# A four-layer macaron network on one core: the third attention's products as single passes over parts, and the first batch's parts of two attentions sent in two steps

## The chip, the cores and the metric

The kernel runs on one core of one Trainium2 chip. The metric is the device time of one execution in microseconds (us). All four layers are one program, so the time is that of the whole network, and the edited stage is about a fifth of it.

## The reference

The state `x` has 4 x 512 x 128 values in f32. Each of four layers adds half a feed-forward block, an attention and the other half of a feed-forward block:

```python
x = x + 0.5 * L3_ffn(x)     # the pattern of every layer, here the last
x = x + L3_attn(x)
x = x + 0.5 * L3_ffn(x)
```

Layers 0 and 3 have mixtures of experts with a limited capacity, layers 1 and 2 other mixtures. The attentions of layers 0, 1 and 3 are softmax attentions with 16 heads of 8 values; layer 2 has a gated recurrence in that place. In the order of time, the attention of layer 0 is the first (its tiles end in `a0`), that of layer 1 the second (`a1`), that of layer 3 the third (`a3`). The edited one is the third:

```python
xn = (x - mu) / sqrt(var + eps) * gamma + beta
q, k, v = split(xn @ W_qkv.T + b_qkv)          # 16 heads of 8
scores = q @ k.T / sqrt(8)                      # 512 x 512 for each of 4 x 16 heads, no mask
out = x + (softmax(scores) @ v) @ W_out.T + b_out
```

The first attention has a causal mask and a bias that depends on the distance, the third has neither.

## The kernel before

**Stages.** The state stays on the core in four tiles `xs[b]` (one for each batch, 128 partitions x 4 tiles of tokens x 128). In the third layer, experts write their rows to a table in memory (`res_f`); `combine(b)` loads a batch's rows (`r_f`) and adds them to `xs[b]` (L548 group). `begin(b)` of the attention goes on from there: sums for the norm (`bn_stats`, `bn_aggr`), a power on POOL, the normed rows, four transposes on PE (called T in the prediction) into `nT`, then the products for q and k (`qk`), then those for v, which `values` copies from PSUM into `vpad`, a tile with the 8 values of each head and a column of ones that gives the sum of the softmax's denominators.

**Units.** `attention()` is one function for the first and the third. It runs 16 units (batch b, group g of four heads), one after the other. A head has a slot of 32 rows of the 128 (`SLOT`), and the four products of a unit's four heads run on four row groups of the PE array at once. `bank(...)` gives one of the eight PSUM banks (128 x 512 f32) in turn.

In the third attention a unit computes its scores twice. `largest` makes scores with queries on the partitions (`s_a`, L627) and DVE reduces each bank to the negated maximum of each row (`low<-s_a`, L726). `lowered` transposes these maxima on PE (`low_a`) and DVE adds them to q, giving `ql_a` (L735): q's slot then holds the query's 8 values, and in a row that k keeps at one, minus the maximum. `by_key` makes the scores again with keys on the partitions (`t_a<-ql_a,k_a`, L627), now with the maximum already taken off; ACT takes the exponential straight from the bank into `w_a` (L746), and `times_values` multiplies with `vpad` into `acc_a` (L842). `summed` copies the finished `acc_a` to `ou_a`, `normalized` transposes it (`ot_a`, L861) and divides, `gathered` and `ended` do the output projection (`proj_a`) of a batch and add it to `xs[b]` (`residual`).

**Order.** The order of PE, DVE, ACT and POOL inside `attention()` is written out by hand (`manual_schedule`). A unit is eight half-steps, each a round of two score products of a later unit and two products by key of the present one, taken alternately, with half of the value products behind it:

```python
together(step(largest, n + lead), step(by_key, n))
if of:
    times_values(*((0, NT - 2, 1) if of == (0, NT - 1) else (*of, 0)))
```

`lead = 2 * NT + 2` says that the scores are ten half-steps (one unit and two) ahead of the products by key. Around the rounds, `go_on()` and `begin_next(u)` advance a later batch's `begin(b)` and the routing of the next mixture (`lg`, `rank_f`) by one step at a time, so that these lie between the rounds. `start(u)` makes a unit's q and k, `fetch` (used by the first attention only) loads them. The first unit has an order of its own (`first_unit`), since nothing runs beside its first scores.

**q and k of a unit.** In the third attention `heads` makes q and k of a batch for all heads in an order in which each slot holds a head of each group; `unit_q` (ACT, L1024) and `project` (POOL, L1704) mask them to the unit's group with the constants `own` and `next_row`, and products are f32. In the first attention `split_heads` makes each of q and k as two parts, `hi` (rounded to the format FR, which PE reads in a single pass) and `lo` (the remainder). `to_units` writes the parts to memory as rows of 4 copies x 8 values for each head, in the orders

```python
halves = (0, 1, 0, 1), (0, 0, 1, 1)
```

for q and k, so that one product over a slot's 32 rows sums all four pairs of parts: eight DMAs for a batch (`qrows_a`, `krows_a`, L1091), and `unit_qk` fetches a unit's q and k (L1100). The first unit of the first attention takes another way (`first_qk`, straight from a product with repeated weights).

DMAs are issued on SP's queue unless another engine is named (`nc.scalar` is ACT's, `nc.gpsimd` POOL's).

## Time and profile before

| | us |
|---|---|
| three runs, median (lowest to highest) | 1475.67 (1471.78 to 1477.84) |
| the profiled execution's own time | 1481.44 |
| its span | 1479.7 |
| PE busy | 1231.3 (83%) |
| DVE busy | 889.6 (60%) |
| POOL busy | 693.9 (47%) |
| ACT busy | 680.3 (46%) |

The mean granted clock of PE is 0.907 of full speed. The stages of the profiled execution, read from tables of busy time by stretches (us):

| stretch | stage | PE busy | DVE | ACT | POOL | clock |
|---|---|---|---|---|---|---|
| 0 to 104 | first mixture | 78.5 | 37.8 | 35.9 | 55.8 | 0.98 |
| 104 to 121 | head of the first attention | 7.3 | 6.6 | 1.9 | 2.8 | 0.60 |
| 121 to 320 | its units | 180.5 | 154.1 | 156.6 | 160.5 | 0.97 |
| 970 to 1047 | mixture ahead of the third attention | 63.2 | 31.5 | 24.9 | 35.4 | 0.92 |
| 1047 to 1064 | head of the third attention | 7.3 | 4.5 | 4.3 | 7.4 | 0.50 |
| 1064 to 1357 | its units | 288.9 | 214.4 | 162.3 | 71.5 | 0.98 |
| 1357 to 1395 | its last projection and the next routing | 9.5 | 9.3 | 1.4 | 12.0 | 0.54 |
| 1395 to 1462 | last mixture | 62.9 | 29.4 | 25.4 | 29.9 | 0.95 |

How to read it: a row of a table of stretches gives the busy time of each engine with the number of instructions in brackets. A row of the timeline gives start, duration, engine, line of the kernel, operation, and output<-inputs, and in brackets how long the engine had waited and for whom. A group's row gives the total, the mean of one in ns, and the idle time ahead of it. Each engine runs its own instructions in the order written, and waits where an input is not there or an output's buffer is not free. L627 is the line of `product`, so products of scores and by key are told apart by their tiles.

### The profile page before, as it was taken

The page shows a single profiled execution, that of the slowest core. Times are in us where ns is not written, and L with a number is a line of the kernel's source. Part 1 is how long each engine was busy: PE and PEld are TensorE (multiplying, and loading weights), DVE is VectorE, ACT ScalarE, POOL GpSimd, SP SyncE. Part 2 cuts the span into 40 slices and gives each one's busy share as a digit, 9 for nine tenths or more (in the row PEclk, how much of TensorE's full clock was granted, in tenths as well). Part 3 has the DMA queues.
Part 4 walks back from the last instruction along what each step waited for, and adds up shares of the span by engine and source line. Part 5 has one row for each costly group of instructions (what it writes and reads, how often), then busy time and mean ns, then how long its engine had stood idle before and what let it go on. Part 6 is the DMA issues. An engine that isn't in the chain of part 4 may idle for free.

```text
span 1479.7 us, 27632 instructions
## 1 busy us (share of the span) xinstructions
PE 1231.3 (83%) x9882; PEld 770.7 (52%) x9882; DVE 889.6 (60%) x3109; ACT 680.3 (46%) x1434; POOL 693.9 (47%) x812
## 2 busy tenths in 40 slices
PE   5877999977979899989898688359599999997494
PEld 4554776765746566666564344237343434332273
DVE  5236888753356676776468867434488787771252
ACT  2334977852442477767521112123256655553041
POOL 5545878862524777777332113645421242213253
PEclk9997999996999999999999777579799999998597
DMA  8623333103433674420220810132100000000333
GB/s 260 193 58 107 123 105 108 38 18 104 123 81 103 177 254 137 140 84 17 58 58 1 301 44 12 34 103 73 39 16 8 9 15 2 15 1 16 79 85 109
DMA packets 109548, 122.40 MB, mean 83 GB/s; under 512 B 10038, under 2 KB 74788, under 8 KB 109412
## 3 DMA queue, kind: packets, MB, share of 16 engines
q1 hardware_dynamic: 97892, 103.22, 23.9%
q0 software_dynamic: 6656, 13.22, 2.7%
q10 hardware_dynamic: 4864, 4.20, 1.0%
q8 instruction: 79, 1.29, 0.3%
q14 instruction: 57, 0.47, 0.1%
HBM read 70.36 MB, written 50.24 MB: 82 GB/s over the span
## 4 chain that ended last, share of the span: by engine, by line
PE 62%; DVE 14%; POOL 8%; issue 7%; DMA 6%; ACT 3%; SPq 0%; POOLq 0%; ACTq 0%; DVEq 0%
PE s_a L627 11%; PE t_a L682 8%; PE h_f L496 5%; PE o_f L532 5%; PE acc_a L842 5%; PE acc_a L704 4%; DVE x L1588 3%; PE t_a L627 3%; PE gu_f L1356 2%; PE y_f L1557 2%; PE gu_f L1357 2%; POOL disp_f L422 2%; PE o_f L1391 2%; PE ot_a L861 2%; POOL res_f L518 2%
## 5 line engine op out<-in xcount | busy, mean ns | idle before, releaser
L669 POOL TENSOR_SCALAR sc_a<-sc_a,top_a 128x128 f32<-128x128 f32 (+3 forms) x256 | 275.9, 1092 | 74.9 <-DVE top_a L654 38.5
L627 PE MATMUL s_a<-k_a,q_a 32*128 32x512 f32 (+3 forms) x1280 | 239.6, 536 | 14.3 <-DVE top_a L658 6.6
L726 DVE TENSOR_REDUCE low<-s_a 128x1 f32<-128x512 f32 x256 | 163.1, 684 | 42.8 <-PE t_a L627 30.6
L746 ACT ACTIVATE w_a<-t_a 128x512 f32<-128x512 f32 x240 | 131.9, 596 | 108.8 <-PE t_a L627 72.2
L682 PE MATMUL t_a<-ident,sc_a 128*128 128x128 f32 x1280 | 170.8, 279 | 7.1 <-DVE top_a L658 6.5
L518 POOL DMA_INDIRECT res_f<-y_f,back_f x112 | 106.8, 953 | 135.5 <-ACT y_f L517 108.1
L682 PEld LDWEIGHTS t_a<-ident,sc_a 128*128 128x128 f32 x1280 | 142.4, 143 | 32.8 <-issue 12.0
L627 PE MATMUL t_a<-ql_a,k_a 32*128 32x512 f32 x480 | 159.0, 644 | 0.6 <-DVE low L726 0.4
L671 ACT ACTIVATE sc_a<-sc_a,top_a 128x128 f32<-128x128 f32 (+3 forms) x256 | 134.3, 577 | 17.8 <-DVE top_a L658 12.4
L627 PEld LDWEIGHTS s_a<-k_a,q_a 32*128 32x128 f32 x1280 | 84.9, 185 | 84.1 <-issue 45.8
L691 ACT ACTIVATE w_a<-t_a 128x256 f32<-128x256 f32 (+2 forms) x192 | 94.4, 527 | 60.8 <-PE t_a L682 60.1
L422 POOL DMA_INDIRECT disp_f<-n_f,to_f x96 | 95.1, 991 | 44.5 <-issue 32.4
L532 PE MATMUL o_f<-w_l,h_f 128*128 128x128 f32 (+1 forms) x896 | 110.2, 278 | 2.4 <-ACT h_f L500 2.3
L496 PE MATMUL h_f<-dT_f,w_l 128*128 128x320 f32 (+1 forms) x256 | 106.4, 554 | 2.8 <-ACT dT_f L474 2.8
L532 PEld LDWEIGHTS o_f<-w_l,h_f 128*128 128x128 f32 (+1 forms) x896 | 102.3, 184 | 11.4 <-ACT h_f L500 4.3
L704 PE MATMUL acc_a<-w_a,vpad 128*32 128x128 f32 x2560 | 97.5, 278 | 0.7 <-ACT w_a L691 0.6
L693 ACT COPY w_a<-t_a 128x256 f32<-128x256 f32 (+2 forms) x192 | 93.6, 528 | 5.8 <-PE t_a L682 5.8
L173 POOL TENSOR_SCALAR rs_f<-mv_f 128x4 f32<-128x4 f32 (+1 forms) x23 | 5.3, 232 | 184.5 <-DVE mv_f L170 184.3
L658 DVE CUSTOM_DVE_ANT_0 sc_a<-s_a,future 128x128 f32<-128x128 f32 (+3 forms) x128 | 62.3, 487 | 44.8 <-PE s_a L627 39.8
L517 ACT ACTIVATE y_f<-o_f,d_f 128x128 f32<-128x128 f32 (+1 forms) x112 | 39.0, 394 | 106.4 <-DVE o_f L512 99.6
L842 PE MATMUL acc_a<-w_a,vpad 128*32 128x256 f32 x1024 | 83.7, 398 | 2.3 <-ACT w_a L746 2.0
L1403 POOL TENSOR_TENSOR h_f<-h_f,cb_f 128x512 f32<-128x512 f32 x32 | 40.6, 1285 | 80.1 <-DVE h_f L1362 41.5
(366 smaller groups left out, 2210.1 us busy)
## 6 DMA issues: line engine op xcount, KB each, us to landing
fac_a<-fac_a_sb SPq DMA_DIRECT2D x36, 256.0 KB
disp_f<-zeros_f SPq DMA_DIRECT2D x4, 2080.0 KB
d_f<-disp_f SPq DMA_DIRECT2D x32, 260.0 KB
w_l<-in_L_ffn_w_dram SPq DMA_DIRECT2D x16, 512.0 KB
cb_f<-rows_f SPq DMA_DIRECT2D x16, 512.0 KB
q_a<-fac_a SPq DMA_DIRECT2D x32, 256.0 KB
k_a<-fac_a SPq DMA_DIRECT2D x32, 256.0 KB
r_f<-res_f SPq DMA_DIRECT2D x16, 256.0 KB
```

Source lines behind the costliest of these rows:

```text
L422: nc.gpsimd.indirect_dma_start(out=self.to[c][i0 + t][:, :], out_offset=bass.IndirectOffsetOnAxis(ap=to[:, c, t : t + 1], axis=0), in_=ns[ ...
L496: nc.tensor.matmul(ps[u][:, :cap], w1[:, e, (c + u) * P : (c + u + 1) * P], dT, start=True, stop=True)
L518: nc.gpsimd.indirect_dma_start(out=self.back[e * per + s][:, :], out_offset=bass.IndirectOffsetOnAxis(ap=back[:m, s : s + 1], axis=0), in_ ...
L532: nc.tensor.matmul(po[:m, s, :], h[:, c, s * P : s * P + m], w2[:, e, c, :], start=(c == 0), stop=(c == NC - 1),)
L627: nc.tensor.matmul(ps[:, n0:n1], q[r : r + SLOT, i * P : (i + 1) * P].bitcast(as_), k[r : r + SLOT, n0:n1].bitcast(as_), start=True, stop= ...
L669: nc.gpsimd.tensor_scalar(sc, sc, top, None, ALU.subtract)
L671: nc.scalar.activation(sc, sc, AF.Exp, bias=top, scale=-1.0)
L682: nc.tensor.transpose(ps[:, x * n + j * P : x * n + (j + 1) * P], st["sc", u, i, r0 + x][:, j * P : (j + 1) * P], ident,)
L704: nc.tensor.matmul(st["acc", u][r * SLOT : (r + 1) * SLOT, i * P : (i + 1) * P], vpads[b % 2][:, j, g * 4 + r, :], st["w", u, i, r][:, j * ...
L726: nc.vector.tensor_reduce(st["low", u][:, i, c : c + 1], ps, AX.X, ALU.max, negate=True)
L746: nc.scalar.activation(w, ps, AF.Exp)
L842: nc.tensor.matmul(acc[r * SLOT : (r + 1) * SLOT, n0:n1], vpads[b % 2][:, j, g * 4 + r, :], st["w", u, j, r, half] if ("w", u, j, r, half) ...
```

## The change

- **Units from the second on in parts.** The third attention uses the first's method: q and k of a batch come from the plain projection (`split_late`), as `x` (ACT), `hi` (ACT, for the first batch's q DVE) and `lo` (POOL, for the first batch's q DVE); `to_units` writes them to memory and `fetch` loads each unit's q and k, three units ahead. Score products and products by key are then single passes in FR. `unit_q`, the masked k, `heads`, `head_weights`, `own` and `next_row` go.
- **The largest in parts.** In a unit of parts q's slot is full, so minus the maximum can't be a row of it. `top_in_parts` splits the maxima into two FR parts in columns 0 and 1 of a slot of `low` (two small operations on DVE, one unit ahead); `lowered` copies the transposed tile into `less` on ACT in place of the addition on DVE; `by_key` adds to each bank a second product, of `twos` (ones in rows 0 and 1 of each slot) with `less`. `by_key_half`, used in the first unit only, stays as it was.
- **The first unit** stays f32, on q and k of its own (`first_plain`), whose weights are zero outside its rows, with a row of ones from the bias.
- **The order.** `lead` becomes `2 * NT + 4`; `first_unit` makes two more half-steps of scores and fetches unit 3; `top_in_parts(u + 1)` stands at the third step (j = 2) of unit u; `begin(b)` of the later batches gets two more yields.
- **Work that changes engine** in the third attention: the additions of `combine` (DVE to POOL for batches 1 to 3), the copies of v (DVE to ACT for batches 1 to 3; v's bias is now folded into the row `ob` by a product in the weights' preparation), the copy `oT` (to ACT).
- **Two steps.** For the first batch of the first and the third attention `to_units` writes group 1 first (eight DMAs of 64 KB, q's on SP's queue and k's on ACT's), then groups 2 and 3 (eight of 128 KB, on SP's); group 0 is not written. All other batches are written whole, as eight DMAs of 256 KB on SP's queue.

```diff
+        two = pool.tile([P, 2, P], FP, name="two", tag="two", bufs=1)
+        nc.gpsimd.memset(two[:, 0], 0.0)
+        for r in range(4):
+            nc.gpsimd.memset(two[r * SLOT : r * SLOT + 2, 0, :], 1.0)
+        nc.gpsimd.tensor_copy(two[:, 1].bitcast(FR), two[:, 0])
...
             for ps, r in out:
-                c = r * SLOT + (units[u][1] + 1) % NG * HD
-                nc.vector.tensor_reduce(st["low", u][:, i, c : c + 1], ps, AX.X, ALU.max, negate=True)
+                nc.vector.tensor_reduce(st["top", u][:, i, r : r + 1], ps, AX.X, ALU.max, negate=True)
+
+        def top_in_parts(u):
+            low = lows[u % len(lows)].rearrange("p t (r c) -> p t r c", c=SLOT)
+            hi, lo = (low[:, :, :, x] for x in range(2))
+            nc.vector.tensor_copy(hi.bitcast(FR), st["top", u])
+            nc.vector.tensor_tensor(lo, st["top", u], hi, ALU.subtract)
...
+            if in_parts(u):
+                st["less", u] = pool.tile([P, S], FP, name=f"less_{tag}{u}", tag="less", bufs=2)
+                nc.scalar.copy(st["less", u].bitcast(FR), ps)
+                return
...
-                yield lambda ps=ps, r=r: product(ps, k, st["ql", u], r * SLOT, j, 0, S)
+                yield lambda ps=ps, r=r: product(ps, k, q, r * SLOT, j, 0, S, as_, True)
                 out.append((ps, r))
+            for ps, r in out:
+                rows = slice(r * SLOT, (r + 1) * SLOT)
+                yield lambda ps=ps, rows=rows: nc.tensor.matmul(
+                    ps, twos[0][rows, :].bitcast(FR), st["less", u][rows, :].bitcast(FR), start=False, stop=True
+                )
...
-        lead = 2 * NT + 2
+        lead = 2 * NT + 4
...
+                        if j == 2 and nxt:
+                            top_in_parts(u + 1)
                         together(step(largest, n + lead), step(by_key, n))
...
+    def to_units(parts, tag, first=False):
+
+        out = [
+            dram.tile([NG, 4, 4, HD, S], FP, name=f"{name}rows_{tag}", tag=f"{name}rows_{tag}") for name in "qk"
+        ]
+        for g0, g1 in ((1, 2), (2, NG)) if first else ((0, NG),):
+            for (hi, lo), order, rows, queue in zip(parts, halves, out, (nc.sync, nc.scalar if g0 == 1 else nc.sync)):
+                for x in (0, 1):
+                    for c in (c for c in range(4) if order[c] == x):
+                        queue.dma_start(
+                            rows.rearrange("g h c d s -> c (g h) d s")[c, g0 * 4 : g1 * 4],
+                            (hi, lo)[x][g0 * SLOT : g1 * SLOT],
+                        )
...
-                qk[b] = to_units(split_heads(pool, nT, wT, bT, tag), tag, (nc.sync, nc.sync if b else nc.scalar))
+                qk[b] = to_units(split_heads(pool, nT, wT, bT, tag), tag, b == 0)
...
-                yield from summed(b)
+                yield from summed(b, nc.gpsimd if b else nc.vector)
...
-                    if t == 1:
+                    if t == 1 or b > 0 and t < NT - 1:
                         yield
...
-                qk[b] = heads(pool, nT, mixed, bT, tag)
+                if b == 0:
+                    whole_[:] = first_plain(pool, nT, first, tag)
+                rows[b] = to_units(split_late(pool, nT, wT, bT, tag, b == 0), tag, b == 0)
                 yield
-                values(b, nT, wvT, bv, tag)
+                values(b, nT, wvT, None, tag, b > 0)
```

The new function that makes the parts in the third attention (behind the products for q and k, `ps`):

```python
            nc.scalar.activation(x, ps[s], AF.Identity, bias=bT[:, s : s + 1])
            if first and s == 0:
                nc.vector.tensor_copy(hi.bitcast(FR), x)
            else:
                nc.scalar.copy(hi.bitcast(FR), x)
            (nc.vector if first and s == 0 else nc.gpsimd).tensor_tensor(lo, x, hi, ALU.subtract)
```

## The prediction

> **What bounds the kernel now.** I read the page first, then stretches of time, then single half-steps in order of time. The whole-span shares (PE 83%) are an average over stages, so I start from the stage that is edited: the third attention, from its first score product at 1063.7 us to its last value product at 1357 us. Busy us of each engine there (columns: start:end, length, PE, PEld, DVE, ACT, POOL, granted clock, DMA share, GB/s):

> ```profile
> 1270.00:1290.00 20.00, 19.79 (x157) 7.02 (x159) 13.42 (x23) 11.04 (x21) 10.19 (x11) 1.00 0.09 28
> 1290.00:1310.00 20.00, 20.00 (x183) 7.67 (x179) 15.58 (x29) 12.94 (x25) 0.00 (x0) 1.00 0.01 1
> 1310.00:1330.00 20.00, 20.00 (x171) 8.05 (x170) 15.47 (x39) 11.40 (x22) 3.84 (x10) 1.00 0.00 1
> 1345.00:1362.00 17.00, 12.83 (x72) 5.22 (x72) 1.79 (x5) 4.93 (x9) 2.40 (x3) 0.77 0.04 13
> ```

> PE is full at full clock, DVE stands at 13 to 16 of 20, ACT at 11 to 13. So PE's work sets the pace. The sixteen units (batch, group) end with a copy ou_a; those copies run from 1095.0 to 1357.0 us, so 15 units take 262.0 us, 17.5 us each. What a unit consists of, in the groups and then in one half-step (two score products and two products by key, on four row groups of the array at once):

> ```profile
> L726 DVE TENSOR_REDUCE low<-s_a 128x1 f32<-128x512 f32 x256 | 163.1, 684 | 42.8 <-PE t_a L627 30.6
> L746 ACT ACTIVATE w_a<-t_a 128x512 f32<-128x512 f32 x240 | 131.9, 596 | 108.8 <-PE t_a L627 72.2
> ```
> ```profile
> 1129.06 0.69 PE L627 MATMUL s_a<-k_a,q_a 32*128 32x512 f32 x1
> ...
> 1129.59 0.59 PE L627 MATMUL s_a<-k_a,q_a 32*128 32x512 f32 x1
> ...
> 1130.13 0.64 PE L842 MATMUL acc_a<-w_a,vpad 128*32 128x256 f32 x8
> 1130.22 1.29 DVE L726 TENSOR_REDUCE low<-s_a 128x1 f32<-128x512 f32 x2 [0.60 <-PE t_a L627]
> 1130.26 1.08 ACT L746 ACTIVATE w_a<-t_a 128x512 f32<-128x512 f32 x2 [0.80 <-PE t_a L627]
> ...
> 1130.70 0.69 PE L627 MATMUL s_a<-k_a,q_a 32*128 32x512 f32 x1
> ```

> Each f32 product is two instructions, 0.53 us apart, so a round of four products takes 1.07 us (1129.06 to 1130.13); the value products follow for 0.57 (to 1130.70). DVE and ACT wait for PE (0.60 and 0.80 in brackets). The first attention already runs its products in single passes, and shows what one costs:

> ```profile
> 211.27 0.45 PE L627 MATMUL s_a<-k_a,q_a 32*128 32x384 f32 x4
> 211.65 0.41 PE L379 MATMUL rank_f<-masks_f,not_before 128*128 128x32 f32 x2
> ...
> 215.22 0.51 PE L627 MATMUL s_a<-k_a,q_a 32*128 32x512 f32 x4
> 215.66 0.66 PE L682 MATMUL t_a<-ident,sc_a 128*128 128x128 f32 x4
> ```

> A round of four at 512 columns holds PE for 0.44 us (215.22 to 215.66), at 384 for 0.38. The slope, 0.055 per 128 columns, makes about 0.22 of pure streaming in 512.

> **The change part by part, stage sum first.** Per half-step PE loses 1.07 and gains 0.44 for the four products, plus the two new products of `twos` with `less` that add to the same banks. No row shows these. Below, they cost the stream alone, 0.22; above, a round of their own, 0.44. I take 0.31, since an f32 pair spends 0.53 on two double streams (0.44) and thus about 0.09 above its streaming. So 0.75 in place of 1.07.

> In the 262 us there are 118 half-steps with products by key (472 instructions t_a). Values take 120 x 0.57 = 68, the transposes ot_a and low_a 15 x 2 x 0.59 = 18, and PE's batch work (T, qk, v, proj, routing) and waits the remainder. Batch work by its rows: 5.8 qk, 3.5 v, 3.5 proj, 3.2 lg, with transposes and ranks about 22. That leaves 262 - 68 - 18 - 22 = 154 for products, or 1.30 a half-step: 1.07 and 0.23 of slips, of which the trace shows 0.25 in every other half-step (1127.17 to 1128.49 is 1.32, not 1.07). After: 118 x 0.75 = 89, so PE's floor is 89 + 68 + 18 + 22 = 197.

> DVE's floor: about 196 busy in these 262 us. Off go 14 additions ql_a (9.6), five batch sums of 0.84 moved to POOL (4.2), values and q of three batches (2.1 + 2.3), about 1.4 of copies; on come 14 splits of the largest, two small operations each, with 0.17 to 0.25 by the 0.16 to 0.26 us of DVE's other small rows: 5 to 7. About 183. ACT: 151 busy, minus 13 masked q (9.6), plus 14 copies `less` at 0.59 and for three batches some 2.8 each: 158. POOL loses 12 masked k (9.2) and gains about 12 additions at 1.27, and has room (0 to 10 of 20).

> PE and DVE now stand close, so waits between them count. Eight banks hold one sum and four products per half-step; in the built order the fourth product of every other half-step in the first half of a unit, and sometimes the third, waits for the reduce of the half-step before. A half-step starting at P has its first score in DVE's hands at P + 0.6, both reduced at P + 1.85 (two at 0.61 and a wake-up); a tight next round, due at P + 1.32, then finishes its products at about P + 1.85 + 0.55 rather than P + 2.07: about 0.35 late. With four tight ones per unit that is 1.4 a unit, 21 over 15: pace 197 + 21 = 218, or 14.5 a unit. Ends: 197 (no waits) and, all tight, two half-steps per 2.94 + 0.08, 8 x 1.51 + 1.2 + 1.5 = 14.8 plus DVE's 2.7 of other work not hidden, 17.5.

> **Queues and head of the third attention.** Batch 1 must be rearranged through DRAM before unit 4. In the built order only the v products and four half-steps, 1.0 + 4 x 1.45 = 6.8 us, stand on PE between its projection and its first use; unit 4 is started a half unit earlier than in the kernel before, which needed no DRAM trip here. In the first attention the same eight writes and the fetch run on SP so:

> ```profile
> 148.38 1.17 SPq L1091 DMA_DIRECT2D qrows_a<-qhi_a  x2
> ...
> 157.49 0.33 SPq L1100 DMA_DIRECT2D k_a<-krows_a  x1
> ```

> 9.1 us from first write to the fetch of k, about 2.5 more to land (writes to fetch in the same rows: 154.4 to 157.5 is 3.1), and 1.4 ahead for two ACT operations: 13.0. PE is blocked for 13.0 - 6.8 = 6 us, and everything queued behind it on PE (products by key, values) waits too; SP's next loads are for later units and don't matter. All later batches have one and a half units, 21 us, and are free. PE falls to a lower clock after such a gap: 130 to 160 us, behind the 6.44 below, has 0.85. I add 2. The head: four more projections of f32 ahead of the first scores, 1.9 us in the warm second set of the first attention (118.44 to 120.3), against 0.9 saved in v at the better clock: 1.4 in all. POOL's six small fills for `two` (0.2 each) follow its fills of low (974.81), after which POOL waits 13.87 us for the first expert anyway; without that wait, about 1 us. Total loss 9.4.

> **First attention, two steps.** PE waits here for unit 1:

> ```profile
> 134.35 0.48 PE L627 MATMUL s_a<-k_a,q_a 32*128 32x128 f32 x4 [6.44 <-DMA k_a<-krows_a]
> ```

> The wait for eight writes of 256 KB becomes one for eight of 64 KB, but eight more writes (128 KB) are issued on SP, 0.6 each, ahead of the fetch: it moves from 128.8 to about 127 at best 125. Gain 0 to 4.5, I take 2.5; next in line behind it is POOL, which is busy until 132.3.

> Sum: 262 - 218 = 44, minus 9.4, plus 2.5: 37 saved. The profiled execution took 1481.4 (span 1479.7 and 1.7 around), so 1444 by its clock; it lies 5.8 above the median of 1475.67, on which I forecast **1439**.

> [...] DVE's row above waits for PE, and in 1290 to 1310 it is 78% busy: it has a quarter to give. [...] And where PE waits, the clock counts: the row 1345 to 1362 has PE 75% busy at 0.77. [...]

> **Rivals.**
> (a) Emptying PSUM binds: all half-steps tight, part of DVE's other work unhidden, 16 us a unit. 262 - 240 = 22, minus 9.4, plus 2.5: 1461. For: DVE's floor of 183 is close to PE's 197, and waits in both directions. Against: the second half of each unit has banks to spare in the built order. Chance 0.2.
> (b) The products don't come in at one pass: the added pair costs a round of its own (0.44) and the old slips of 0.23 stay. 118 x (0.88 + 0.23) + 108 = 239: 1460. For: no row shows the pair; against: rounds of 0.44 in all ten units that I looked at. Chance 0.1.
> (c) Slower: PE's clock gives way in the stage. At clock c its floor is 197/c; with 9.4 lost and 2.5 won it passes 262 from c below 0.77. At 0.75 it is 263 plus waits of 10: 1475.7 + 273 - 262 + 6.9 = 1494. For: 75% busy goes with 0.77 above. Against: the first attention at 36.52 of 40 (200 to 240 us) keeps 1.00, and the after-stage should be 90% busy. Chance 0.1.
> (d) No waits at all: 197, so 1418. Chance 0.1.

> **Numbers.** The forecast has 0.5. About 0.5% (7.4 us) is what a measurement of this kernel can tell from no change. (a), (b) and (d) are faster by more than that, but for 0.08 that falls short through their upper ends (17.5 a unit): faster 0.82, same 0.08, slower 0.10. The range takes in (d) and the far side of (a): 1414 to 1468.

> **What would show it.** Right: ou_a copies about 14.5 us apart; reduce pairs of 1.29 back to back; `less` products adding about 0.3; PE blocked once for some 6 us by k_a<-krows_a of batch 1; the wait at 134.35 shorter by 2 or 3. Wrong: copies still 17 apart with PE waiting for DVE top_a (then a), full PE with longer rounds (b), or a clock under 0.9 in the stage (c).

## The result, and the profile after

The changed kernel takes 1465.27 us (median of 21 runs, 1446.72 to 1482.56) against 1475.67 (21 runs, 1468.56 to 1481.09): 10.4 us or 0.7% less by the medians, where 37 us (2.5%) were forecast. The ratio on record, 0.9885 (interval 0.9863 to 0.9906), leaves out eight of the changed kernel's 21 runs, those more than 1.5% above its fastest. The profiled execution took 1471.50 (span 1469.8), 9.9 less than that of before and 6.2 above the median.

The third attention's stretches after (columns as before; behind the engines stand granted clock, DMA share and GB/s); the last row is the stretch from the first copy ou_a to the last:

```profile
1120.00:1140.00 20.00, 13.35 (x106) 5.39 (x105) 10.01 (x18) 9.15 (x18) 7.42 (x6) 0.74 0.49 157
1140.00:1160.00 20.00, 20.00 (x142) 7.39 (x140) 12.61 (x26) 10.98 (x21) 0.00 (x0) 0.58 0.09 28
...
1280.00:1300.00 20.00, 20.00 (x205) 8.70 (x201) 17.67 (x34) 16.62 (x31) 0.83 (x1) 1.00 0.11 34
...
1320.00:1347.00 27.00, 26.96 (x151) 10.63 (x150) 2.85 (x15) 11.99 (x22) 8.20 (x10) 0.50 0.06 21
...
1103.06:1347.01 243.95, 232.54 (x1896) 100.83 (x1896) 169.36 (x407) 156.96 (x291) 72.82 (x106) 0.84 0.20 63
```

PE looks full in three of the first four rows, but the clock, 1.00 from 1074 to 1350 us in the profile before, stands at 0.58 and 0.50 in two of them. The copies ou_a run from 1103.06 to 1347.01, 16.3 us apart in the mean. At full clock the five steps from 1242.34 to 1310.44 are 13.6 each in the mean (14.0 with the one ahead of them, from 1226.23, which is at full clock too), and units without a batch's work 11.8 to 12.2. One half-step at full clock and one at half, with the two long waits for DMA and one for DVE (timeline of the changed kernel):

```profile
1081.24 0.76 PE L633 MATMUL s_a<-k_a,q_a 32*128 32x512 f32 x1 [3.23 <-DMA k_a<-krows_a]
...
1132.03 0.76 PE L633 MATMUL s_a<-k_a,q_a 32*128 32x512 f32 x1 [6.65 <-DMA k_a<-krows_a]
...
1144.95 0.79 PE L633 MATMUL s_a<-k_a,q_a 32*128 32x512 f32 x1
...
1145.55 0.63 PE L768 MATMUL t_a<-less_a,two 32*128 32x512 f32 x2
...
1146.11 1.08 PE L872 MATMUL acc_a<-w_a,vpad 128*32 128x256 f32 x8
...
1211.27 0.50 PE L633 MATMUL s_a<-k_a,q_a 32*128 32x512 f32 x1
...
1211.60 0.40 PE L768 MATMUL t_a<-less_a,two 32*128 32x512 f32 x2
1211.93 0.64 PE L872 MATMUL acc_a<-w_a,vpad 128*32 128x256 f32 x8
1212.50 0.49 PE L633 MATMUL s_a<-k_a,q_a 32*128 32x512 f32 x1
...
1216.72 0.50 PE L633 MATMUL t_a<-q_a,k_a 32*128 32x512 f32 x1 [1.21 <-DVE top_a L738]
```

At full clock the four single passes take 0.33 (1211.27 to 1211.60), the pair with `less` 0.33 and the values 0.57: 1.23 in all. At half clock (1142.79 to 1144.95) the same costs 2.16. A microsecond of such half-steps at half clock thus loses 1 - 1.23/2.16 = 0.43.

**When the clock falls.** In this stretch of the trace it changes ten times from 1085 us on, always between 1.00 and 0.50, and all ten changes lie on one grid of 3.41 us, as closely as bins of 0.1 us tell. So I cut the trace on that grid. Four windows (1.00 in the first, second and fourth, each followed by 0.50; 0.50 in the third, followed by 1.00):

```profile
1126.02:1129.44 3.42, 0.00 (x0) 0.00 (x0) 0.40 (x2) 0.00 (x0) 1.48 (x2) 1.00 0.94 312
1194.29:1197.70 3.41, 3.31 (x32) 1.82 (x35) 2.29 (x8) 2.26 (x6) 0.00 (x0) 1.00 0.00 0
1201.12:1204.53 3.41, 3.41 (x22) 1.62 (x20) 2.57 (x7) 1.09 (x2) 0.00 (x0) 0.50 0.02 5
1310.34:1313.76 3.42, 3.32 (x32) 1.83 (x35) 2.30 (x8) 2.24 (x6) 0.00 (x0) 1.00 0.00 0
```

The first is the wait for batch 1. In the second and fourth PE is busy for 97%, yet the clock falls; from 1115.78 to 1119.20 PE is busy for 75% (2.55 us), and it stays. Busy time does not separate these windows, but the work in them does. I count a product as its share of the array's 128 x 128 cells times its columns over 512, an f32 instruction twice (four value products of 256 columns, begun at 1211.93 in the changed kernel, are followed by the next four 0.24 us later; a full-array single pass of 512 takes 0.24 too, 5.74 us for 24 in the run with the wait filled): "passes". The second and fourth window hold the routing's eight products of 8 columns (`lg_f`, 1.06 us of PE), next to nothing in passes. At full clock the five windows ahead of a fall hold 5.5 passes or less, the 47 others 5.8 or more. At half clock the five ahead of a rise hold 5.8 or more; of the 20 others all but one or two hold less, and those 5.8 to 6.0 (some records of products are missing, so a count is good to a few per cent). At the 0.22 us that the prediction reads for 512 columns, 3.41 us have room for 15.5 passes, so 5.5 and 5.8 are 0.35 and 0.37 of a full array by this estimate; the expectations below speak of about 0.35.

The same count between the first and the last copy in all fourteen traces gives 46 windows ahead of a fall, with 5.84 passes at most, and 735 at full clock that stayed up, of which four hold less than 5.8 (4.3 to 5.7). PE was busy for 90% or more in 11 of the 46, and for less in 28 of the 735. At half clock the two groups overlap: 47 of 50 windows ahead of a rise hold 5.8 or more, but so do 20 of the 169 others (up to 6.2).

By this count the clock can stay down by itself, as for 27.3 us behind batch 1. A half-step has 1 pass of scores and products by key, 0.5 of `less`, 2 of values: 3.5. At half clock a window holds 3.41/2.16 = 1.58 of them, 5.5 passes, where the windows ahead of a rise hold 5.8 or more; each of the four rises between the first and the last copy (1112.4, 1156.8, 1204.6 and 1221.6) stands behind a window with one of the transposes `ot_a` and `low_a` (2 passes each; begun at 1111.59, 1155.79, 1202.99 and 1220.95). Before, the f32 products made it 4 + 2 = 6 passes per half-step of 1.64 us, so at half clock, if it took twice that time, a window would hold 3.41/3.28 x 6 = 6.2 by this estimate: more than 5.8.

The first attention's wait (PE, then SP's queue):

```profile
136.76 0.48 PE L633 MATMUL s_a<-k_a,q_a 32*128 32x128 f32 x4 [8.63 <-DMA k_a<-krows_a]
```
```profile
124.83 1.90 SPq L1120 DMA_DIRECT2D qrows_a<-qhi_a  x2
126.77 2.24 SPq L1120 DMA_DIRECT2D qrows_a<-qlo_a  x2
129.13 1.32 SPq L1120 DMA_DIRECT2D krows_a<-khi_a  x2
130.56 1.19 SPq L1120 DMA_DIRECT2D krows_a<-klo_a  x2
131.79 0.82 SPq L1131 DMA_DIRECT2D q_a<-qrows_a  x1
132.66 0.59 SPq L1131 DMA_DIRECT2D k_a<-krows_a  x1
```

The wait is 8.63 in place of 6.44. Unit 1's k is fetched at 132.66, behind the second step's eight writes, 2.8 later than before (129.88).

### The profile page after: what moved, and what is told of

Same layout as the page of the kernel before. It is cut to its first block, busy times and chain, and to the rows that moved or that the text cites. A ratio compares the mean times of both kernels' runs of the same rounds, so it can differ in the third digit from the quotient of the medians.

```text
span 1469.8 us, 27370 instructions
## 1 busy us (share of the span) xinstructions
PE 1209.4 (82%) x9649; PEld 775.7 (53%) x9649; DVE 874.5 (60%) x3109; ACT 689.7 (47%) x1450; POOL 699.2 (48%) x818
## 4 chain that ended last, share of the span: by engine, by line
PE 58%; DVE 17%; DMA 8%; POOL 7%; issue 4%; ACT 3%; SPq 1%; POOLq 0%; ACTq 0%; DVEq 0%
PE t_a L691 7%; PE o_f L532 6%; PE s_a L633 6%; PE h_f L496 6%; PE acc_a L872 5%; PE acc_a L713 4%; DVE x L1619 3%; DVE top_a L738 2%; PE y_f L1588 2%; PE t_a L768 2%; PE gu_f L1387 2%; DVE sc_a L667 2%; PE gu_f L1388 2%; POOL disp_f L422 2%; PE ot_a L891 2%
## 5 line engine op out<-in xcount | busy, mean ns | idle before, releaser
L633 PE MATMUL s_a<-k_a,q_a 32*128 32x512 f32 (+3 forms) x1040 | 168.6, 491 | 24.6 <-DMA k_a<-krows_a 18.5
L738 DVE TENSOR_REDUCE top_a<-s_a 128x1 f32<-128x512 f32 x240 | 151.5, 683 | 34.7 <-PE s_a L633 23.3
L633 PEld LDWEIGHTS s_a<-k_a,q_a 32*128 32x128 f32 x1040 | 69.8, 189 | 101.7 <-issue 51.3
L872 PE MATMUL acc_a<-w_a,vpad 128*32 128x256 f32 x1024 | 96.7, 458 | 0.0
L633 PE MATMUL t_a<-q_a,k_a 32*128 32x512 f32 x240 | 82.6, 571 | 4.0 <-DVE top_a L738 3.3
```

The lines of the kernel that those rows point to most:

```text
L633: nc.tensor.matmul(ps[:, n0:n1], q[r : r + SLOT, i * P : (i + 1) * P].bitcast(as_), k[r : r + SLOT, n0:n1].bitcast(as_), start=True, stop= ...
L738: nc.vector.tensor_reduce(st["top", u][:, i, r : r + 1], ps, AX.X, ALU.max, negate=True)
L872: nc.tensor.matmul(acc[r * SLOT : (r + 1) * SLOT, n0:n1], vpads[b % 2][:, j, g * 4 + r, :], st["w", u, j, r, half] if ("w", u, j, r, half) ...
```

## The experiments

The theory, from the counts above: the clock falls, and stays down, by the work per window; DMA waits and late DVE or routing work start a fall. The rivals are in the expectations. Chips differ: the kernel before took 1474.5, 1487.6, 1491.0 and 1487.6 us in the four groups, so ratios to its runs on the same chip are given. Of each edit the lines that matter are shown; "..." marks what is left out.

**Unit 1 fetched ahead of the second step.**

```diff
+            if g0 == 1 and between is not None:
+                between(out)            # fetches unit 1's q and k
...
```

> Both first batches still leave in two steps, but unit 1's q and k are fetched right behind the first step, ahead of the second step's eight writes on SP's queue. Queue theory (the fetch is late because it stands behind those writes): in the first attention PE's wait for k falls from 8.63 us to about 3, in the third from 3.23 to nothing; with the clock that is kept, 6 to 10 us less in all. Rival (the landing of the first step's writes sets the fetch, not the queue): both waits stay within 1 us and so does the time.

Measured: 1459.97 us, ratio 0.9915 (0.9885 to 0.9944).

```profile
135.02 0.48 PE L633 MATMUL s_a<-k_a,q_a 32*128 32x128 f32 x4 [5.68 <-DMA k_a<-krows_a]
```

The wait in the first attention falls to 5.68, not 3 (the fetch of k still stood behind three of the second step's writes of q, and left at 132.10); that in the third falls from 3.23 to 0.61. So the queue it is. The 6 to 10 us less were not seen: the ratio is not told apart from that of the changed kernel, and the clock still falls at batch 1 and at unit 7. Behind batch 1 it is down for only 6.8 us here, after a wait of 5.94, against 27.3 in the changed kernel. The first full window behind the wait happens to take in most of the transposes ot_a and holds 6.0 passes, where that of the changed kernel holds 5.6. So in these two runs the length of the fall (6.8 and 27.3 us) went with where the grid lay.

**The wait filled.** A small function adds products of a loaded k with itself to the next bank, before it is written:

```diff
+            if "fill" in st:
+                other, n = st.pop("fill")
+                for _ in range(n):
+                    nc.tensor.matmul(ps, other[:, :P].bitcast(FR), other.bitcast(FR), start=True, stop=True)
...
+                        if now and (24 * (n + 0 + lead == 32)):
+                            fill(u, 24 * (n + 0 + lead == 32))
```

> The 6.65 us in which PE waits for batch 1's k at unit 4 are filled with 24 products of 512 columns over the full array, whose results are overwritten; the wait itself stays. Clock theory (the clock is judged in windows of 3.41 us by the work that the array did, and falls where that is under about 0.35 of a full array's): the clock stays at 1.00 behind the wait, the 27 us at half clock go, which at 2.16 against 1.23 us a half-step is 11 to 12 us less. Rival (the single-pass stream itself can't hold the clock, wait or no wait): the clock falls within the next two units all the same, and the time is that of the changed kernel or up to 2 us more.

Measured: 1453.80 us, ratio 0.9867 (0.9828 to 0.9906). Timeline of this run, and the 27 us that were at half clock in the changed kernel:

```profile
1124.70 5.74 PE L639 MATMUL s_a<-k_a 128*128 128x512 f32 x24
1131.06 0.50 PE L640 MATMUL s_a<-k_a,q_a 32*128 32x512 f32 x1 [0.62 <-DMA k_a<-krows_a]
```
```profile
1129.44:1156.78 27.34, 25.71 (x247) 10.76 (x246) 23.04 (x50) 19.39 (x36) 4.62 (x9) 0.99 0.21 68
```

The wait is as long as before and the clock holds. From the copy of unit 1 to that of unit 3 it takes 29.5 us in place of 39.7: 10.2 less, from a wait that still ends when k lands. That is what this fall cost, apart from the wait that starts it. Some of it is lost again: unit 4 takes 18.7 us here against 17.2, with a fall of 3.4 us at 1156, and the ratio is not told apart from the changed kernel's 0.9885.

**One added product in every half-step.** The condition is `now` alone, one product each.

> One added full-array product of 512 columns in each half-step of the third attention from unit 1 on, result overwritten. Clock theory: the array's work per window stays over 0.35, so the clock is at 1.00 in the tail too and returns within two windows of a wait; about 120 x 0.22 = 26 us of products come on, some 84 us at half clock go (36 us): 10 us less than the changed kernel. Rival (the clock gives way to power or to idle time, not to a lack of work): clock in the stage stays near 0.83 and the time is 26 us more.

Measured: 1476.46 us, ratio 1.0021 (1.0002 to 1.0039).

```profile
1146.00:1340.60 194.60, 194.26 (x1692) 88.99 (x1691) 150.62 (x359) 131.06 (x243) 54.65 (x85) 1.00 0.18 59
```

The clock did as the theory said: from 1146 us to the copy of unit 14 it never falls. The time did as neither said: a single added product among those on 32 rows takes 0.42 (1201.53 to 1201.95), not 0.22, and a unit without batch work grew from about 12.0 to 14.2.

**The products as f32.**

```diff
-                return *parts[units[u]], FR
+                return *parts[units[u]], FR if added else FP
```

> As the changed kernel, but the products of q and k are read as f32 (two instructions each) again; the product with less stays. Clock theory: half-steps last 1.07 + 0.33 + 0.57 = 1.97 us, the clock is at 0.97 or more outside the waits for DMA, as in the kernel before; about 17.5 us a unit, and 15 to 20 us more than the changed kernel. Rival (the new order and its waits lower the clock, not the single passes): the clock falls in the same places, 0.83 in the stage, and the time is 40 us or more above the changed kernel.

Measured: 1506.97 us, ratio 1.0205 (1.0176 to 1.0234).

```profile
1142.00:1387.00 245.00, 243.42 (x2126) 103.23 (x2120) 155.91 (x369) 141.15 (x261) 59.83 (x90) 1.00 0.16 49
```

Same order, and no fall between the copies but at the wait for batch 1 (5.03 us), where it lasts two windows (6.8 us) instead of eight. That length alone decides nothing, since the first experiment has it too; that no other fall comes is the point. So in these runs the other falls come with the single passes. The edit does more than that, though: with longer half-steps PE's waits for DVE (0.55 and 1.21 in the changed kernel) are gone too, so this run alone does not tell whether falls are not started or do not last. The time is nearer the rival's number, since a unit took 18.4 (copies from 1107.63 to 1384.28), not 17.5; the clock decides against it.

**Batch 1 begun earlier.** Six `begun(1)` in `first_unit`, on top of the first experiment:

```diff
             together(top[6], first[0, 1])
+            begun(1)
             together(top[7], first[0, 0])
+            begun(1)
...
```

> Batch 1 of the third attention is begun in the first unit (six of its steps), so that its projection stands five half-steps earlier, and the first batches' unit 1 is fetched ahead of the second step's writes, as in the experiment before. Queue theory: PE's wait at unit 4 (5.94 us in that experiment) falls under 1 us, its cold stretch behind it goes, and against that experiment 6 to 10 us are saved: about 1451. Rival (another wait takes its place: DVE, busy with the first unit's reduces, or POOL make batch 1 late all the same): the wait stays above 4 us and the time is 1458 or more.

Measured: 1462.43 us, ratio 0.9829 (0.9807 to 0.9852). The wait at unit 4 is gone; from the first copy to the fourth it takes 40.2 us in place of 60.0 (41.1 in its second run, below; the trace here is of an execution of 1488.76 us). Later falls remain.

**Added products at chosen places, first try.**

> As the experiment with the early batch 1, and 20 added full-array products of 512 columns at the places where the traces so far showed windows under 0.35 (first half of unit 1, the routing products of 8 columns at units 6, 10 and 14, waits for DVE at units 4 and 7); results overwritten. Clock theory: no fall of the clock from unit 2 to the end, about 13.6 us a unit; 4 us of products come on, two or three cold stretches of 7 to 27 us go: 5 to 12 us less than with the early batch alone, and less scatter from run to run. Rival (falls are not set by the work in a window): the same falls, 4 us more.

Measured: 1474.06 us, ratio 0.9897 (0.9864 to 0.9931), 11.6 us more than the early batch alone on this chip, where 5 to 12 less were expected and the rival said 4 more. It failed: the routing's products stand one half-step behind where I put these, and the clock still fell there (1185) and at units 7 and 11.

**The first attention whole again.** `to_units` of its first batch writes whole pieces on two queues.

> As the changed kernel, but the first attention's first batch is written whole on two queues, as before. Queue theory: PE's wait in the first attention is 6.4 us again in place of 8.63, and the first attention's units take 1 to 2 us less; the third attention is as in the changed kernel. Rival (writing in two steps helps there by itself): the wait grows beyond 8.6.

Measured: 1480.91 us, ratio 0.9972 (0.9944 to 1.0001). The wait is 6.59; from the head's transposes to the first unit's copy it takes 34.2 us against 36.7 in the changed kernel and 34.3 before. At the end of the first attention 0.4 us of those 2.5 are left, not the 1 to 2 that were expected; what takes up the rest stays open.

**The sums on DVE again.** `yield from summed(b, nc.vector)`, with the early batch 1.

> As the experiment with the early batch 1, but the sums of combine run on DVE again in all batches. The trace of the changed kernel shows DVE waiting 0.94 us for POOL's sum (behind POOL's indirect transfers) with the reduces queued behind it, and PE 1.21 us for those, in the window before a fall of the clock at unit 7. Wait theory: PE's waits of over 1 us at units 7 and 11 go, and with them the falls there: 4 us of DVE come on, 8 to 15 us go, ratio to the kernel before 0.975 to 0.98. Rival (DVE is the bound there, and the sums on it only lengthen the waits): the falls stay, and the time is that of the early batch or 5 us more.

Measured: 1470.07 us, ratio 0.9862 (0.9826 to 0.9898).

```profile
1202.59 0.79 PE L633 MATMUL t_a<-q_a,k_a 32*128 32x512 f32 x1 [1.44 <-DVE top_a L738]
...
1268.25 0.50 PE L633 MATMUL t_a<-q_a,k_a 32*128 32x512 f32 x1 [1.46 <-DVE top_a L738]
```

My theory fell here: with the sums on DVE the waits are 1.44 (unit 7) and 1.46 (unit 11), where the early batch alone has 1.19 and 1.42 (in its second run, below, with one more of 2.46 for ACT's copy `less` at unit 7 and one of 1.95 for DVE at unit 11). So it is not POOL's sums that make these waits, as the rival says; that DVE sets the pace there is not shown by that alone. DVE and ACT have little slack beside single passes. In a half-step at full clock DVE is busy for 1.21 of 1.23 us and ACT for all of it (changed kernel), though between the first and the last copy they are busy for 169 and 157 of 244 us:

```profile
1211.27:1212.50 1.23, 1.23 (x18) 0.46 (x14) 1.21 (x3) 1.23 (x3) 0.93 (x2) 1.00 0.16 54
```

**Added products at the routing's place**, on top of that.

> As the run before it in this list, and 8 full-array products of 512 columns ahead of unit 1's transposes of the maxima, and 2 in each half-step of j = 1 in units 4, 6, 10 and 14, where the routing's products of 8 columns stand (the experiment with added products at the first try had them one half-step too early); results overwritten. Clock theory: no fall in the windows with the routing's products, tail at full clock; 24 products cost 6 us at most, and with two to three cold stretches less the time is 3 to 10 us under that of the run before it. Rival: the same falls, 6 us more.

Measured: 1477.95 us, ratio 0.9923 (0.9896 to 0.995). No fall at the routing, as the theory said, but those at units 7 and 11 lasted 27 and 24 us, and the time went up by 7.9 us. In the run before they lasted 10 and 24 us, so the products themselves and a longer fall at unit 7 may both have cost it; the traces do not part the two.

**Control, early batch, and added products where a fall has to be ended**, three kernels on one chip; the last:

```diff
+                            fill(u, 1 if u in (6, 10, 14) and j == 1 else 2 if u in (7, 11) and j > 1 or u in (8, 12) and j == 0 else 0)
```

> The changed kernel itself, as a control on the chip of the next two. Both theories: about 0.9885 of the kernel before. Clock theory: its runs scatter by 2% and their time falls with the mean clock, some 0.4 us for each us that the clock is not at half; rival (other causes of scatter): no such relation.

> The early batch 1 with unit 1 fetched ahead of the second step's writes, once more on the chip of its neighbours. Queue theory: 8 to 15 us under the changed kernel (two waits of 3.2 and 6.6 us, one in the first attention shorter by 2.8, and the cold stretches behind them). Rival (falls elsewhere take the place of those removed): within 5 us of it.

> As the early batch 1, and 30 added full-array products of 512 columns, results overwritten: one in each half-step of j = 1 in units 6, 10 and 14 (routing), two in each of the six half-steps from j = 2 of units 7 and 11 on, where DVE is late and the clock falls. Clock theory: with 5.5 in place of 3.5 full passes in a half-step the clock is back one or two windows after a fall; cold stretches of 17 to 35 us there become 7 or less; 7 us of products against 12 to 20 us: 5 to 12 us under the early batch alone. Rival (a fall lasts whatever work is added): 7 us more than it.

Measured: 1488.29 (ratio 1.0008, 0.998 to 1.0037), 1472.34 (0.9892, 0.9852 to 0.9933) and 1460.45 (0.9834, 0.9802 to 0.9865). The stretches from unit 10 on, the early batch first, then with added products:

```profile
1260.00:1280.00 20.00, 16.52 (x116) 6.62 (x112) 10.24 (x19) 9.00 (x17) 6.71 (x7) 0.73 0.18 54
1280.00:1300.00 20.00, 20.00 (x124) 7.64 (x124) 11.23 (x20) 10.40 (x19) 0.00 (x0) 0.50 0.00 1
1300.00:1320.00 20.00, 19.65 (x173) 9.62 (x170) 16.00 (x36) 12.46 (x23) 3.84 (x10) 0.91 0.01 1
```
```profile
1260.00:1280.00 20.00, 18.43 (x128) 7.80 (x126) 10.39 (x20) 8.79 (x17) 6.41 (x7) 0.83 0.17 53
1280.00:1300.00 20.00, 19.74 (x198) 8.95 (x194) 17.91 (x40) 15.76 (x30) 1.52 (x3) 1.00 0.01 2
1300.00:1320.00 20.00, 20.00 (x188) 9.60 (x188) 14.20 (x45) 14.00 (x27) 3.83 (x10) 1.00 0.00 1
```

The fall at unit 11 lasts 6.8 us in place of 34.1, and the one at the routing of unit 14 (1320.6 in the early batch) does not come. At unit 7, with as many added products, it lasts 13.7 in place of 17.1: a return within one or two windows was seen at unit 11 only. Thirty products whose results nobody reads make the kernel 11.9 us faster than the early batch and 27.8 faster than the changed kernel on the same chip, and it is faster than the kernel before there (0.9834).

The control was not faster than the kernel before on that chip, where about 0.9885 was expected: the small gain of the change does not show there. Its time at half clock is longer (median 383 us, twice one minus the clock, times the span; in the 21 runs 352); its trace has the falls at batch 1, at the routing of unit 6 and at unit 7 again, and two more (13.7 us at unit 7, 27.3 at unit 11). Why there is more of it on that chip stays open.

## Why the prediction was wrong, point by point

**The step that failed is the clock**: "PE falls to a lower clock after such a gap ... I add 2." From the first copy to the last, 80.1 us ran at half clock (9.3 at unit 1, 27.3 behind batch 1, 6.8 and 3.4 at units 6 and 7, 33.2 in the tail), at 0.43 each 34 us, an estimate from one half-step at each clock (1.23 and 2.16 us). I took the price of one fall from 130 to 160 us, where the stage had other products, and did not ask what brings the clock back. Behind batch 1 alone the fall cost 10.2 us (run with the wait filled, whose wait is as long).

**The sum with measured terms.** Pace 13.6 x 15 = 204 (forecast 218), wait for batch 1 6.65 (6), clock 34 (2): 245, where the copies show 243.95. That this closes is in part my choice of steps: at 14.0, with the step ahead of those five, the pace is 211, and 27 are left for the clock. Either way the clock is the term that was off by far the most. The head of the third attention lost 6.7 (1.4): from its transposes to the first copy 46.0 us against 39.3. I had not priced a wait for unit 1's k there (3.23); with that nearly gone (first experiment) it is 44.1, so the wait is 2 of the 6.7. The clock was at half for 22.1 us in that stretch, against 11.6 before; at 0.43 the 10.5 more make 4.5, an estimate that would account for the rest. The first attention lost 1.1 from its transposes to its last copy (forecast a gain of 2.5). Against the forecast that is -14 + 0.7 + 32 + 5.3 + 3.6 = 27.6; 1444.4 by the profile's clock becomes 1472.0, and 1471.5 was measured.

**What held.** The pair with `less` cost 0.33 (0.31). The products and the pair took 0.66 in place of 0.75, and the old slips of 0.23 are down to about 0.1 in units without batch work. The wait for batch 1 is there, and as long as forecast. DVE's floor was 183, from 196 busy between the copies; the profile before has 188 there, and after it is 169. So the single passes did what I took them for, and a little more (pace 204 to 211, forecast 218); most of their gain was given back by the clock.

**The two steps.** I saw the eight writes ahead of the fetch and gave them too little: I took 127 for the fetch, and it left at 131.8 for q and 132.66 for k. The sign was wrong.

**The rivals.** (c) had the mechanism: its 197/c, with 0.84 for c over the units, gives 235, and 241 with the wait. I gave it 0.1 and only the case below 0.77. (a) had nearly the number, 16 us a unit and 1461, but by luck: PE's waits for DVE exist (1.21 us), yet at full clock the pace was 13.6 to 14.0. In the tightest half-steps DVE and ACT, which empty the banks, do have no time left: from 1211.27 to 1212.50 DVE is busy for 1.21 of 1.23 and ACT for all of it. Waits for DVE of 1.2 to 1.5 us also stand right ahead of falls, at unit 7 in the changed kernel and the first experiment and at unit 11 with the sums on DVE; other falls at unit 7 follow a wait for ACT's copy `less`, or none that stands out. (b) and (d) did not come.

**The scatter** bears the same sign: over the 21 runs the time rises by 0.38 us for each us at half clock (306 to 397 us, correlation 0.985), and by 0.32 (0.94) in the control's. The kernel before has 266 to 308 in the runs of the four groups.

## What to carry to other kernels

Here the cheaper products left the clock down: a window of half-steps at half clock holds 5.5 passes, and 47 of the 50 windows ahead of a rise hold 5.8 or more. So before making products cheaper, read from the kernel's own trace what the windows hold on either side of each change of the clock, work out what one would hold at half clock with the new products, and if that is too few, ask what will lift the clock again. Price a wait with the time that the clock stays down behind it (here 6.65 us of waiting, and 10.2 lost behind it; less where the grid lay otherwise), and fill it or end it early. Where a transfer is cut in two, look at what is queued between the first part and what waits for it: here PE's wait was 8.63 us with the fetch behind the whole second step, 5.68 with it ahead of most of that, and 6.59 with the batch written whole.
